# A vision tower in one program: last updates of layer 0 one per pair, and another order of work at the end of layer 1

## The chip, the cores and the metric

The kernel runs as one program on one core of a Trainium2 chip. The core has a matrix engine (TensorE, PE in the views), a vector engine (VectorE, DVE), a scalar engine (ScalarE, ACT), a general-purpose one (GpSimd, POOL) and SyncE (SP), which issues transfers (DMAs). Each engine works through its own list of instructions in order, and waits only on semaphores. TensorE writes to PSUM, of which the kernel uses eight banks; everything else lies in SBUF. The metric is the device time of one execution in microseconds (us). The profile's span, from the first instruction to the last, is somewhat shorter than that time: 1984.1 us against 1985.91 us in the profiled execution.

## The reference

32 images of 3 x 256 x 256 are cut into 256 patches each, and each patch becomes a vector of 256 numbers. Two layers follow, all in float32:

```python
h = _L0_tok_ref(x, L0_tok_W, L0_tok_b)
h = h + _L0_attn_ref(_layernorm(h, axis=-1), ...)
h = h + _L0_ffn_ref(_layernorm(h, axis=-1), ...)
h = h + _L1_attn_ref(_layernorm(h, axis=-1), ...)
h = h + _L1_ffn_ref(_layernorm(h, axis=-1), ...)
```

Three of these matter here. Layer 0's feed-forward ranks the 256 tokens of an image by a learnt weight, runs the best 127 through two matrices, and adds the results, times the weight, back at their places. Layer 1's attention is causal, over phases: two small networks, a product of phases, and a running sum. Layer 1's feed-forward has four heads with four causal experts each: softmax attention per expert, a gate that mixes the four results, a residual and a norm, two small matrices (fc1, fc2) with another norm, and a softmax over heads that scales the result:

```python
gs = jax.nn.softmax(jnp.einsum('bnsf,nef->bnse', out, gate_w) + gate_b[None, :, None, :], axis=-1)
mixed = jnp.einsum('bnsed,bnse->bnsd', out.reshape(b, nh, s, ne, d), gs)
hn = layernorm(mixed + resid, ln_g, ln_b)
...
fg = jax.nn.softmax(fout @ fgate_w.T, axis=-1)
return (fout.reshape(b, s, nh, d) * fg[..., None]).reshape(b, s, h)
```

## The kernel before

All 32 images stay in SBUF (tiles h0 to h31, two chunks of 128 tokens by 256). The stages run one after the other: patches, layer 0's attention in pairs of images, layer 0's feed-forward in quads, layer 1's attention in pairs, layer 1's feed-forward image by image. Within a stage the work of several images is interleaved, and the order of instructions on TensorE, VectorE, ScalarE, GpSimd and SyncE is the order in which the code records them; nothing is moved afterwards. So a line of the loops says for every engine at once where a piece of work stands in its queue.

**Layer 0's feed-forward, its end.** `step_c(t)` (L838) runs what the table ORDER_C lists for step t. For the last quad (images 28 to 31) three steps are left when the stage ends: END_C has `fetch` of the first half; END_C + 1 `fetch` of the second half and `update` of the first; END_C + 2 `update` of the second. `fetch` (L810) issues four gathers on GpSimd (L816), which bring an image's two chunks of results to the order of its tokens. `update` (L821) has, for two images of two chunks, three VectorE instructions each: multiply and add to h (L827), and statistics for the next norm (L123, L124); then two small GpSimd instructions turn variances into reciprocal roots (L148, L149).

**Layer 1's attention** (L966 to L1006) is a loop over t in which each pair of images starts three steps after the one before. `do(k, which)` runs a piece k steps after its pair's start: at 0 `norm_d` (VectorE, L774 to L777, makes dx), at 1 `turn` (TensorE transposes dx, L188; ScalarE copies one half to dxT, L193, VectorE the other, L195) and `residual_d` (GpSimd, L786 and L787), at 2 `hidden` (matmuls with w_wk and w_wq, activations), at 3 `phases` (L901 to L906), at 4 `match` (matmuls on dz; VectorE multiplies by the causal mask, L921), at 5 `memory` (dat,dx), at 6 `output` (matmuls wvo,dm, then statistics on VectorE, L945 and L946, and GpSimd's power d_rs), at 7 `add_output` (L955, which also frees the four banks of `output`) and `stats_e`. A step with t a multiple of 3 ends with `output`; the next one begins with `turn`. The three steps of layer 0 are run at the ends of t = 6, 7 and 8.

**Layer 1's feed-forward.** `prep` and `values` do the attention. `post(b, im, i)` (L1179) has the rest of image b in pieces i: 0 to 2 the gate (logits L1185 to L1192, softmax, then L1199 and, on GpSimd, two products of expert results and gate, L1202), 3 the mixed sum er (L1207 to L1210), 15 its squares on ScalarE (L1171), 4 their sum (L1215) and GpSimd's power (L1153, L1154), 5 the scaling (L1220), 6 the transposes (L750) and fxT (L1224), 16 a count of zeros in fxT (L1066), 7 fc1, hx (L1233) and four copies by SyncE into the tile both (L1237, L1239), 8 the matmuls with fc2 and ey (L1248), 9 and 10 squares, sum and power, 11 the scaled enorm (L1256) and the logits of the last gate, 12 transposes and foT (L1268), 13 transposes back (L1276), 14 the rest of the softmax, the product into the tile fout (L1281), the addition of h (L1285) and the output by SyncE (L1286). The pool p1 has one buffer for each name: er, fxT, hx, both, enorm, foT, fout and ex (the normed input, L754) among them. After the loop, when the last image's attention is done, the table END lists the pieces that are left as (images back from the last, piece), and

```python
for back, i in END:
    post(B - 1 - back, images[B - 1 - back], i)
```

records them in that order. Piece 10 of every eighth image is followed by `check_ranges` (L1145), two VectorE instructions over 384 numbers; their sum decides, through a flag that TensorE and VectorE finish (L1356 to L1367), whether a general version of the layer is run after all.

Of the kernel before, what the change touches and what calls it, by code (L numbers as in the profile page):

```python
# [33 lines left out]
F32 = mybir.dt.float32  # L34
# [6 lines left out]
P = 128  # L41
B, N, D = 32, 256, 256
NC = N // P
# [36 lines left out]
def vit_tower(tc, a, out):  # L80

    nc = tc.nc
# [34 lines left out]
    def over(ap, shape, axis):  # L117
        return ap.unsqueeze(axis).to_broadcast(shape)
# [422 lines left out]
    p1 = region_c.enter_context(tc.tile_pool(name="c_1", bufs=1, reuse_waits="tile"))  # L541
# [241 lines left out]
    def residual_d(b0, s):  # L783
        for j in range(2):
            h = H[b0 + j]
            nc.gpsimd.tensor_tensor(h, h, s.xs[j], ALU.add)  # L786
            nc.gpsimd.tensor_tensor(h, h, over(add_row, [P, NC, D], 1), ALU.add)  # L787

    with region_c:
# [48 lines left out]
        def step_c(t):  # L838
            for at_step, do, j in ORDER_C:
                u, r = divmod(t - at_step, 4)  # L840
                if r == 0 and 0 <= u < B // 4 and (u > 1 or do is not first_ranks):
                    do(4 * u, quads[u], j)

        END_C = 4 * (B // 4 - 1) + 4
# [20 lines left out]
    with (  # L865
# [3 lines left out]
        def turn(b0, s):  # L869
            s.xT = p2.tile([P, 2, 2 * N], F32, name="dxT")  # L870
            transposed(s.xT, s.xs, copy_split)
# [36 lines left out]
        def match(b0, s):  # L908
            s.t, ps = [], (bank(), bank())
            for key, at_q, w in ((0, 0, N), (P, P, P)):  # L910
                for i in range(2):
                    for j, p in enumerate(ps):
                        r = slice(j * 64, (j + 1) * 64)
                        q = N + at_q
                        mm(
                            p[:, 2 * key : 2 * key + w], s.z[r, i, key : key + P], s.z[r, i, q : q + w],
                            i == 0, i == 1,
                        )
            for p in ps:
                t = p8.tile([P, N + P], F32, name="dat", bufs=4)  # L920
                nc.vector.tensor_tensor(t, p[:, 0 : N + P], causal, ALU.mult)  # L921
                s.t.append(t)
# [14 lines left out]
        def output(b0, s, qs=range(2 * NC)):  # L937
            if qs[0] == 0:
                s.st, s.po = spool.tile([P, 2 * NC, 2], F32, name="d_st"), []
            for q in qs:  # L940
                m, c, p = s.m[q // NC], q % NC, bank()
                for k in range(2):
                    mm(p, m[:, k, c * P : (c + 1) * P], wvo[:, k, :], k == 0, k == 1)
                six = spool.tile([P, 6], F32, name="six")
                nc.vector.bn_stats(six, p[:, 0:D])  # L945
                nc.vector.bn_aggr(s.st[:, q, :], six)  # L946
                s.po.append(p)
            if len(s.po) == 2 * NC:
                s.rs = spool.tile([P, 2 * NC], F32, name="d_rs")
                pow_rstd(s.rs, s.st[:, :, 1])  # L950

        def add_output(b0, s):
            for q, p in enumerate(s.po):
                h = H[b0 + q // NC][:, q % NC, :]
                nc.vector.scalar_tensor_tensor(h, p[:, D:], s.rs[:, q : q + 1], h, ALU.mult, ALU.add)  # L955
# [10 lines left out]
        for t in range(3 * (NP - 1) + 8):  # L966
            def do(step, which, *more):
                u, r = divmod(t - step, 3)
                if r == 0 and 0 <= u < NP:
                    which(2 * u, pairs[u], *more)  # L970

            last = t == 3 * NP + 1
            if t != 4:
                do(1, turn)
            if not last:
                do(7, add_output)
            if t != 4:
                do(4, match)
            if last:
                output(B - 4, pairs[NP - 2], (3,))  # L980
                add_output(B - 4, pairs[NP - 2])
            do(7, stats_e)
            if t != 4:
                do(1, residual_d)
            do(2, hidden, 0)
            if t == 2:
                do(2, hidden, 1)
                turn(2, pairs[1])
            elif t == 5:
                do(2, hidden, 1, (0,))  # L990
                match(0, pairs[0])
                do(2, hidden, 1, (1,))
            else:
                do(2, hidden, 1)
            do(5, memory)
            do(3, phases)
            if t == 5:
                residual_d(2, pairs[1])
            if t > 3:
                do(0, norm_d, p8, "dx", 4)  # L1000
            if t == 3 * NP:
                output(B - 4, pairs[NP - 2], (0, 1, 2))
            else:
                do(6, output)
            if 6 <= t <= 8:
                step_c(END_C + t - 6)  # L1006
    right_d.close()
    passing_x.close()
    by_hand.close()
# [2 lines left out]
    with (  # L1012
# [129 lines left out]
        def in_range(b, first, n):  # L1142
            return ranges[:, b // 8 % 2, b % 8, first : first + n]

        def check_ranges(b):  # L1145
            r = ranges[:, b // 8 % 2, :, :].rearrange("p b x -> p (b x)")
            nc.vector.scalar_tensor_tensor(good, r, 1.0 / LOW, good, ALU.is_le, ALU.mult)
            nc.vector.scalar_tensor_tensor(good, r, 1.0 / HIGH, good, ALU.is_ge, ALU.mult)

        def head_rstd(x):  # L1150

            v = spool.tile([P, NC * NH], F32, name="hv")
            nc.gpsimd.tensor_scalar(v, x, 1.0 / HD, 1e-8, ALU.mult, ALU.add)  # L1153
            nc.gpsimd.tensor_tensor(v, v, minus_half, ALU.pow)  # L1154
            return v
# [7 lines left out]
        def softmax_rest(x, g):  # L1163
            m = spool.tile([P, g], F32, name="sm_m", tag=f"sm_m{g}")
            nc.vector.tensor_reduce(m, x, AX.X, ALU.add)
            nc.vector.reciprocal(m, m)
            nc.vector.tensor_tensor(x, x, over(m, [P, g, 4], 2), ALU.mult)  # L1167
# [6 lines left out]
        def expert_pair(im, k, at, w):  # L1174

            x, step = at[2 * k], at[2 * k + 1] - at[2 * k]
            return im.o[:, :, x : x + 2 * step].rearrange("p g (e x) -> p g e x", e=2)[:, :, :, 0:w]

        def post(b, im, i):  # L1179
# [17 lines left out]
            if i == 2:  # L1197
                softmax_rest(im.gate, NC * NH)
                nc.vector.tensor_tensor(im.gate, im.gate, im.rden, ALU.mult)  # L1199
                im.mix = [expert_pair(im, k, MIX, HD) for k in range(2)]  # L1200
                for k in range(2):
                    nc.gpsimd.tensor_tensor(  # L1202
                        im.mix[k], im.mix[k], over(im.gate[:, :, 2 * k : 2 * k + 2], [P, NC * NH, 2, HD], 3), ALU.mult
                    )
            if i == 3:
# [7 lines left out]
            if i in (4, 10):  # L1213
                ss = in_range(b, NC * NH * (NE + i // 10), NC * NH)
                nc.vector.tensor_reduce(ss, im.sq, AX.X, ALU.add)  # L1215
                im.rs = head_rstd(ss)
                if i == 10 and b % 8 == 7:
                    check_ranges(b)
            if i == 5:
                nc.vector.tensor_tensor(im.r, im.r, over(im.rs, G8, 2), ALU.mult)  # L1220
            if i == 6:
# [54 lines left out]
                        nc.tensor.transpose(im.po[:, o : o + P], im.fT[:, k, c * P : (c + 1) * P], ident)  # L1276
            if i == 14:
                softmax_rest(im.gate, NC)
                y = p1.tile([P, NC, D], F32, name="fout")
                y8 = y.rearrange("p c (n d) -> p (c n) d", d=HD)  # L1280
                nc.vector.tensor_tensor(  # L1281
                    y8, im.po.rearrange("p (g d) -> p g d", d=HD),
                    over(im.gate.rearrange("p c n -> p (c n)"), G8, 2), ALU.mult,
                )
                nc.vector.tensor_tensor(y, y, H[b], ALU.add)  # L1285
                nc.sync.dma_start(out[b].rearrange("(c p) d -> p c d", p=P), y)  # L1286
# [19 lines left out]


        END = (
            (1, 1), (1, 2), (4, 12), (2, 5), (3, 16), (0, 0), (2, 6), (1, 3), (1, 15),
            (1, 4), (0, 1), (3, 8), (3, 9), (0, 2), (1, 5), (4, 13), (4, 14), (3, 10),  # L1310
            (2, 7), (2, 16), (1, 6), (0, 3), (0, 15), (2, 8), (1, 7), (0, 4), (2, 9),
            (3, 11), (0, 5), (2, 10), (1, 16), (0, 6), (1, 8), (1, 9), (0, 7), (1, 10),
            (3, 12), (2, 11), (3, 13), (3, 14), (0, 16), (0, 8), (0, 9), (2, 12), (1, 11),
            (2, 13), (1, 12), (0, 10), (2, 14), (0, 11), (1, 13), (1, 14), (0, 12), (0, 13),
            (0, 14),
        )

        def pieces(t, table):
# [427 lines left out]
```

## Time and profile before

Three timed runs took 1986.39, 1988.32 and 1988.48 us. The profiled execution:

| engine | busy us | share |
|---|---|---|
| PE matmul | 1929.2 | 97% |
| DVE | 1308.7 | 66% |
| ACT | 821.1 | 41% |
| POOL | 721.3 | 36% |

The chain of work that ended last could be followed back only to 1922.9 us, so its shares say little of the span; listed in order of time it is of use for the end. Windows of the span, in the form start:end, length, then busy time and count of each engine, TensorE's granted clock, share and rate of DMA:

```
937.50:958.75 21.25, 21.25 (x92) 11.33 (x87) 9.47 (x22) 11.34 (x15) 0.00 (x0) 1.00 0.00 0
979.80:998.40 18.60, 13.15 (x42) 7.29 (x42) 13.27 (x40) 4.99 (x6) 6.11 (x8) 0.82 0.01 1
1009.87:1030.88 21.01, 21.01 (x90) 11.79 (x88) 11.93 (x36) 8.96 (x12) 7.41 (x8) 1.00 0.00 0
1900.00:1922.00 22.00, 22.00 (x444) 17.95 (x441) 19.87 (x60) 15.81 (x38) 9.94 (x8) 1.00 0.19 51
1922.00:1945.00 23.00, 5.23 (x54) 3.42 (x53) 19.34 (x39) 5.71 (x12) 12.89 (x9) 0.69 0.14 35
1945.00:1965.00 20.00, 12.37 (x120) 8.59 (x120) 14.22 (x43) 6.47 (x12) 7.30 (x8) 0.76 0.27 66
1965.00:1984.10 19.10, 3.46 (x14) 2.23 (x14) 7.30 (x25) 1.02 (x3) 1.44 (x1) 0.50 0.14 45
```

The order of the engines is PE, PE's weight loads, DVE, ACT, POOL. The first and the third line are undisturbed stretches of layer 1's attention: TensorE never stops. A row of a timeline gives start and length of a group of like instructions, the engine, the line of the kernel, output and inputs, shapes and count, and in brackets how long the engine had been idle and who ended that. SPq stands for the time a DMA instruction spends at the head of SyncE's queue, waits included.

### The profile page before, as it was taken

Reading aid. Unit: us, or ns where it says so; the run is one execution under the profiler, and the core shown is the slowest. Engines: PE = TensorE matmul, PEld = TensorE weight load, DVE = VectorE, ACT = ScalarE, POOL = GpSimd, SP = SyncE. Lnnn points to the kernel's source line nnn. Section 1 sums busy time; section 2 is a strip of 40 time slices with the busy share of each in tenths; the row PEclk is TensorE's granted clock in tenths of the full one; section 3 lists DMA queues with packets and bytes.
Section 4 is the critical chain, followed back from the end, with each engine's and each line's share of the span. In section 5 each row is a group of like instructions: output and inputs, shape, how many; then the busy total and the mean of one; then the engine's idle time right before and its main releaser. Section 6 shows DMA issues by size and latency. Waiting matters only on the chain. (4 is left out here: it accounts for less than half of the span.)

```text
span 1984.1 us, 37645 instructions
## 1 busy us (share of the span) xinstructions
PE 1929.2 (97%) x15108; PEld 1372.8 (69%) x15108; DVE 1308.7 (66%) x3605; ACT 821.1 (41%) x1549; POOL 721.3 (36%) x692
## 2 busy tenths in 40 slices
PE   9999999999999999999899999999999999999983
PEld 8886676666667766766555555677777777777762
DVE  2334566666686745334655655568999999999986
ACT  0002222222222122122444444477777777777761
POOL 1223234333332344234333333213443443434343
PEclk9999999999999999999999999999999999999996
DMA  8540000000000142121000000002122121212212
GB/s 300 159 144 1 0 17 32 19 19 17 17 19 14 56 128 80 51 69 40 22 1 1 0 1 0 6 18 55 45 57 53 45 66 45 63 48 55 55 39 60
DMA packets 69813, 95.09 MB, mean 48 GB/s; under 512 B 8576, under 2 KB 51200, under 8 KB 69248
## 3 DMA queue, kind: packets, MB, share of 16 engines
q1 hardware_dynamic: 62912, 75.04, 13.3%
q0 software_dynamic: 6144, 16.79, 2.8%
q8 instruction: 121, 1.98, 0.4%
q10 hardware_dynamic: 576, 0.79, 0.1%
q14 instruction: 60, 0.49, 0.1%
HBM read 46.45 MB, written 20.97 MB: 34 GB/s over the span
## 5 line engine op out<-in xcount | busy, mean ns | idle before, releaser
L1124 ACT ACTIVATE et<-bank 128x512 f32<-128x512 f32 x384 | 202.0, 598 | 73.0 <-DVE bank L1122 72.5
L115 PEld LDWEIGHTS bank<-ev,et 128*64 128x64 f32 x6144 | 197.6, 136 | 33.5 <-issue 21.4
L115 PE MATMUL bank<-ev,et 128*64 128x74 f32 (+1 forms) x6144 | 210.5, 226 | 0.0
L1122 DVE TENSOR_TENSOR bank<-bank,w_tri 128x256 f32<-128x256 f32 (+1 forms) x384 | 172.7, 513 | 51.1 <-PE bank L115 50.5
L1202 POOL TENSOR_TENSOR eo<-eo,gate 128x1024 f32<-128x1024 f32 x64 | 122.7, 1938 | 202.9 <-DVE gate L1199 168.6
L115 PE MATMUL bank<-g,sx 64*128 64x512 f32 (+1 forms) x512 | 191.2, 502 | 3.5 <-ACT g L1082 3.5
L115 PE MATMUL bank<-g,sw 64*128 64x512 f32 (+1 forms) x512 | 189.5, 502 | 0.0
L115 PE MATMUL bank<-tokW,patch 128*128 128x256 f32 x768 | 167.2, 381 | 1.8 <-DMA patch<-in_patches_dram 1.8
L115 PEld LDWEIGHTS bank<-tokW,patch 128*128 128x128 f32 x768 | 146.5, 191 | 23.0 <-issue 2.7
L115 PE MATMUL bank<-bxT,w_wuv 128*128 128x512 f32 x300 | 131.4, 592 | 0.0
L1154 POOL TENSOR_TENSOR hv<-hv,minus_half 128x8 f32<-128x8 f32 x64 | 118.5, 1852 | 5.3
L115 PE MATMUL bank<-wvo,dm 128*128 128x512 f32 x256 | 114.3, 599 | 0.0
L115 PE MATMUL bank<-w_wo,gT 128*128 128x256 f32 x512 | 113.1, 379 | 0.0
L115 PE MATMUL bank<-attn,bv 128*128 128x256 f32 x512 | 113.1, 379 | 0.0
L115 PE MATMUL bank<-w_w,hT 128*128 128x256 f32 x512 | 113.1, 379 | 0.0
L1140 ACT COPY eo<-bank 128x286 f32<-128x286 f32 x256 | 96.0, 422 | 39.0 <-PE bank L115 35.7
L115 PE MATMUL bank<-xsel,w_w 128*128 128x512 f32 x256 | 111.4, 592 | 0.0
L115 PEld LDWEIGHTS bank<-attn,bv 128*128 128x128 f32 x512 | 97.2, 190 | 19.5 <-issue 7.2
L1153 POOL TENSOR_SCALAR hv<-ranges 128x8 f32<-128x8 f32 x64 | 37.4, 585 | 198.6 <-DVE ranges L1215 198.5
L123 DVE BATCH_NORM_STATS2 six<-h 128x6 f32<-128x256 f32 x256 | 105.5, 412 | 4.4
L115 PEld LDWEIGHTS bank<-w_w,hT 128*128 128x128 f32 x512 | 96.6, 190 | 15.3 <-issue 2.9
L115 PEld LDWEIGHTS bank<-w_wo,gT 128*128 128x128 f32 x512 | 97.2, 190 | 13.2
(265 smaller groups left out, 3749.8 us busy)
## 6 DMA issues: line engine op xcount, KB each, us to landing
patch<-in_patches_dram SPq DMA_DIRECT2D x31, 768.0 KB, 4.8
sw<-sx SPq DMA_DIRECT2D x64, 128.0 KB, 2.3
both<-fxT SPq DMA_DIRECT2D x64, 128.0 KB, 2.4
both<-hx SPq DMA_DIRECT2D x64, 128.0 KB, 2.4
out_dram<-fout SPq DMA_DIRECT2D x32, 256.0 KB, 2.5
cs<-ranked SPq DMA_DIRECT2D x32, 128.0 KB, 3.2
results<-cy SPq DMA_DIRECT2D x32, 128.0 KB, 1.7
w_w<-in_w_dram SPq DMA_DIRECT2D x2, 1024.0 KB, 8.5
```

What stands on the lines that cost most here:

```text
L115: nc.tensor.matmul(o, lhsT, rhs, start=first, stop=last)
L123: nc.vector.bn_stats(six, x)
L1122: nc.vector.tensor_tensor(own, own, over(tri, [P, n_e, P], 1), ALU.add)
L1124: nc.scalar.activation(t, p, AF.Exp)
L1140: nc.scalar.copy(im.o[:, c * NH + n, 0:OC], p[:, 0:OC])
L1153: nc.gpsimd.tensor_scalar(v, x, 1.0 / HD, 1e-8, ALU.mult, ALU.add)
L1154: nc.gpsimd.tensor_tensor(v, v, minus_half, ALU.pow)
L1202: nc.gpsimd.tensor_tensor(im.mix[k], im.mix[k], over(im.gate[:, :, 2 * k : 2 * k + 2], [P, NC * NH, 2, HD], 3), ALU.mult)
```

## The change

It has four parts.

1. The three steps left of layer 0's feed-forward run at the ends of t = 6, 9 and 12 of layer 1's attention, not 6, 7 and 8: one step per pair of images, each after `output`.
2. For the last two images (b > B - 3) the two products of L1202 run on VectorE, not on GpSimd.
3. For images 27, 29 and 31 the output is made in the p1 tile named ex; images up to 26, 28 and 30 use fout as before.
4. The table END has another order, with one entry more: for the last image, `check_ranges` is a piece of its own, 17, after piece 11, where it followed piece 10.

Of the order: image 27's transposes now come before image 30's products, and its output (4, 14) after piece 9 of image 29, so behind the copies (2, 7) of image 29 in SyncE's queue, and behind piece 8 of 29. Image 30's squares (1, 9) to power (1, 10) and the transposes of the last three images stand in a slightly different order among each other.

```diff
-            if 6 <= t <= 8:
-                step_c(END_C + t - 6)
+            if t in (6, 9, 12):
+                step_c(END_C + (t - 6) // 3)
...
-                    nc.gpsimd.tensor_tensor(
+                    (nc.vector if b > B - 3 else nc.gpsimd).tensor_tensor(
...
-                if i == 10 and b % 8 == 7:
-                    check_ranges(b)
+            if i == (17 if b == B - 1 else 10) and b % 8 == 7:
+                check_ranges(b)
...
-                y = p1.tile([P, NC, D], F32, name="fout")
+
+                y = p1.tile([P, NC, D], F32, name="ex" if b > B - 6 and b % 2 else "fout")
...
         END = (
-            (1, 1), (1, 2), (4, 12), (2, 5), (3, 16), (0, 0), (2, 6), (1, 3), (1, 15),
-            (1, 4), (0, 1), (3, 8), (3, 9), (0, 2), (1, 5), (4, 13), (4, 14), (3, 10),
-            (2, 7), (2, 16), (1, 6), (0, 3), (0, 15), (2, 8), (1, 7), (0, 4), (2, 9),
-            (3, 11), (0, 5), (2, 10), (1, 16), (0, 6), (1, 8), (1, 9), (0, 7), (1, 10),
-            (3, 12), (2, 11), (3, 13), (3, 14), (0, 16), (0, 8), (0, 9), (2, 12), (1, 11),
-            (2, 13), (1, 12), (0, 10), (2, 14), (0, 11), (1, 13), (1, 14), (0, 12), (0, 13),
-            (0, 14),
+            (1, 1), (4, 12), (4, 13), (1, 2), (3, 16), (0, 0), (2, 5), (2, 6), (1, 3),
+            (1, 15), (0, 1), (3, 8), (2, 7), (1, 4), (3, 9), (0, 2), (1, 5), (3, 10),
+            (2, 16), (1, 6), (0, 3), (0, 15), (2, 8), (1, 7), (0, 4), (3, 11), (3, 12),
+            (0, 5), (2, 9), (4, 14), (2, 10), (1, 16), (0, 6), (1, 8), (1, 9), (0, 7),
+            (2, 11), (1, 10), (3, 13), (3, 14), (0, 16), (0, 8), (0, 9), (0, 10), (2, 12),
+            (1, 11), (2, 13), (1, 12), (0, 11), (0, 17), (2, 14), (1, 13), (0, 12), (1, 14),
+            (0, 13), (0, 14),
         )
```

In the changed program the lines from L1280 on are numbered one higher.

## The prediction

> **What bounds the kernel now.** I read the page first: TensorE is busy 97% of the span and its row of tenths is all nines but for one slice (the 20th) and the last two. So a microsecond can be won only where TensorE stops. The timeline of TensorE around that slice (start, length, engine, line, tiles, count, idle before it and who ended it):
>
> ```profile
> 958.75 1.04 PE L188 MATMUL bank<-ident,dx 128*128 128x128 f32 x8
> 959.72 1.58 PE L115 MATMUL bank<-dz 64*128 64x256 f32 x16
> 961.22 3.70 PE L115 MATMUL bank<-dxT,w_wk 128*128 128x512 f32 x8
> ...
> 972.78 7.13 PE L115 MATMUL bank<-wvo,dm 128*128 128x512 f32 x16
> 985.12 0.80 PE L188 MATMUL bank<-ident,dx 128*128 128x128 f32 x2 [5.20 <-DVE dx L777]
> 986.16 1.65 PE L188 MATMUL bank<-ident,dx 128*128 128x128 f32 x6 [0.25 <-DVE dx L777]
> 987.74 2.93 PE L115 MATMUL bank<-dz 64*128 64x256 f32 x16
> 990.60 4.45 PE L115 MATMUL bank<-dxT,w_wk 128*128 128x512 f32 x8
> ...
> 1009.87 1.04 PE L188 MATMUL bank<-ident,dx 128*128 128x128 f32 x8
> ```
>
> An undisturbed pair of images takes 21.0 us from one L188 to the next (1009.87 to 1030.88 later in the same view). From 958.75 to 1009.87 are two pairs in 51.12 us: **9.1 us are lost here**, 5.45 idle and the rest because the same matmuls run slower for 6 us afterwards. VectorE's timeline says why:
>
> ```profile
> 976.57 0.48 DVE L827 SCALAR_TENSOR_TENSOR h<-cx,w_kept,h 128x256 f32<-128x256 f32 x1 [5.23 <-DMA cx<-results,rank_of]
> ...
> 979.08 0.45 DVE L827 SCALAR_TENSOR_TENSOR h<-cx,w_kept,h 128x256 f32<-128x256 f32 x1
> 979.56 0.43 DVE L123 BATCH_NORM_STATS2 six<-h 128x6 f32<-128x256 f32 x1
> 980.03 0.18 DVE L124 BATCH_NORM_AGGREGATE st_d<-six 128x2 f32<-128x6 f32 x1
> ```
>
> The last update of layer 0 waits for a gather issued one step earlier, and the norm of the next pair (L777), which TensorE transposes, stands behind it on VectorE.
>
> The end is the second stop: in the windows view TensorE is busy 5.2 of the 23 us from 1922 and 3.5 of the last 19.1. Queue, product and chain lines of it:
>
> ```profile
> 1925.22 2.95 DVE L1188 TENSOR_TENSOR lg<-eo,ranges 128x64 f32<-128x64 f32 x2
> ...
> 1928.49 1.22 DVE L1207 TENSOR_TENSOR two<-eo 128x1024 f32<-128x1024 f32 x1
> ...
> 1976.48 0.69 DVE L1281 TENSOR_TENSOR fout<-bank,fgate 128x512 f32<-128x512 f32 x1 [3.97 <-DMA out_dram<-fout]
> ```
> ```profile
> 1914.12 25.92 SPq L1286 DMA_DIRECT2D out_dram<-fout  x2
> 1940.27 1.11 SPq L1237 DMA_DIRECT2D both<-fxT  x2
> ```
> ```profile
> 1942.07 3.02 DMA both<-hx
> ...
> 1972.06 4.33 DMA out_dram<-fout
> ```
>
> L1188 takes 2.95 us for two where it took 0.36 at 1920.95: GpSimd runs its products (L1202) beside it. The output of image 27 (L1286, issued at 1939.65) holds back SyncE's copies for image 29. And image 31 waits for image 30's output to leave the only fout tile.
>
> **What the Trainium skill says.** "GPSIMD Engine Reference", § 3 and § 8: elementwise work on two inputs is about twice as slow as on VectorE, and both share SBUF interfaces. The trace agrees in kind: 1.94 us mean for L1202 against 1.22 for L1207, which has as many elements (1.6 times), and L1188 above. "TensorE: Matmul & The Clock Gate", Part 1: after an idle window of some 3.4 us the clock is halved until work has lasted about as long. Here 5.20 us idle did it (2.93 for 1.58). The same page, engine queue depths: VectorE's queue is strictly first in, first out. The trace shows no overtaking.
>
> **The change, part by part.** Sums are against the profiled span, 1984.1.
>
> (a) *Steps of layer 0's end at 6, 9, 12.* Step 6 (four gathers, 5.0 us on GpSimd after d_rs) stays. Four gathers and the first update go from 7 to 9, the second update from 8 to 12. The 9.1 us go, since each update now finds data gathered a pair earlier. But the new place has a price. By the order of the built program, the 12 instructions of an update stand between the statistics of the output (L946) and the dxT copy (L195) of the next pair; in the old place at step 7 they fell into VectorE's idle time. Four times L827, L123, L124 take 4 x 1.04 = 4.16 us (979.08 to the next one at 980.12). In an undisturbed pair L195 runs at 1011.13 to 1011.79; TensorE's first matmul with dxT starts at 1012.35 and needs only the half that ScalarE copies; the second, 0.92 later at 1013.27 (3.70 for four), needs L195. With the update it can start at 1011.79 + 4.16 + 0.1 = 1016.05: a new wait of **2.8 us, twice**. Behind L195 on VectorE stand L955 (frees banks for the wq matmuls) and L921 (wanted at 1019.32 plus 2.8, ready at 1015.2 plus 4.2): both in time. 2.8 is under 3.4, so I take no loss of clock. On GpSimd the gathers and the two small power operations of the update stand behind d_rs and ahead of the statistics for layer 1's feed-forward and the residuals, which are wanted a pair or more later: nothing. Net **-9.1 + 5.6 = -3.5**. Bounds: no slack at all for TensorE (4.16 twice) gives -0.8; half the wait hidden gives -6.
>
> (b) *Products on VectorE, images 30 and 31.* Four instructions at 1.22 (row L1207) instead of 4 x 2.1 on GpSimd. They fill VectorE, but what slowed L1188, L1167 (1.51 for 0.19) and L1285 (1.58 for 0.69) is gone: 2.6 + 1.3 + 0.9 = 4.8. Both are in the walk below.
>
> (c) *New order and (d) second tile.* Walk of image 31 from 1923.8 (end of L1199 of image 30, alike in both), each term a row of this stage. VectorE now works without gaps until image 31's sum (er): four products 4.9, counts 2 x 0.67, logits 1.1 and 0.6, gate softmax 0.9, two norms of er 1.2, two sums of 2.6, ey 0.7, three L1215 1.8; with two or three waits of 0.1, 17.1: 1940.9, before 1943.5. Then squares 0.7, L1215 0.7, GpSimd's power 2.0 with hand-overs: L1220 at 1944.4, before 1950.55 (there L1215 stood behind ey of image 29, which waited for the held copies). Image 27's output and the count of image 30, which frees fxT, come first: 3.8, then fxT 0.8, fc1 matmuls 2.1 (slow clock), hx 0.75, copies 3.0, matmuls 1.9, ey 0.45: 1957.2, before 1961.6. Squares, L1215 and power 3.6: enorm at 1960.8, before 1967.23. From there VectorE's queue to the last add: enorm block 1.55, range checks 1.1 and 1.0 with small steps, outputs of 29, 30, 31 1.45 + 2.0 + 2.0: 1969.9. Image 31 now waits for image 29's output only (issue to landing 2.2 to 2.5 elsewhere): 0.5. The flag's matmul stands behind image 31's transposes on TensorE: 0 to 1.5, I take 0.5. Last add ends at **1970.9 against 1977.89: -7.0**. What follows (6.2 us to the span's end) stays. Fast clock throughout takes off another 1.9 to 2.4 (-9.4); an output that lands as late as the 4.33 above, with the flag's full 1.5, leaves -5.
>
> The range check (piece 17) now stands behind image 31's enorm instead of ahead of it; its 1.1 us are in the walk; the ex tile was read last by image 31's transposes (before 1885), so taking it costs nothing.
>
> Sum: -3.5 - 7.0 = -10.5, span 1973.6. Timed runs were 1986.39 to 1988.48 (median 1988.32); the profiled one was 1985.91. From the median: **1977.8**.
>
> **Rivals.**
> B: *the update gives back all it freed.* Each of its two places costs 4.5 us (update 4.16 and no slack). For: it is in front of the copy. Against: 1.4 us of slack counted above. Only the end pays: 1981.3.
> C: *TensorE stays fast at the end and half the new wait hides.* -6.0 - 8.5 brings 1973.8. For: at 1954 to 1965 it was fast between gaps of 2 us. Against: 4 us gaps in the walk.
> E: *VectorE becomes the bound of the end, which gains nothing*: products at GpSimd's 1.94 (4 x 0.72 = 2.9), and each of the six powers that GpSimd keeps holds VectorE up by 0.7, as its products did (4.2): 7.1, only (a) pays, 1984.8. Against: L1220, also with a broadcast input, keeps L1209's rate (0.69), and beside the power at 1933.03 VectorE's small steps kept their 0.17 to 0.20.
> D, slower: *each update stall is long enough to halve the clock.* L827 ran at 1.16 for 0.45 while GpSimd added two inputs; four such add 2.8 to the stall, 5.6, and the slow clock 3.65 as seen at 985 (9.1 - 5.45): 9.25 a step. 18.5 - 9.1 - 7.0 = +2.4: 1990.7. It decides for slower from 8.05 a step on. Against: at that place GpSimd runs powers and gathers, beside which L827 took 0.45 (966.00).
>
> **How the numbers follow.** Forecast 0.70, B 0.13, C 0.07, E 0.06, D 0.04. A measurement can tell about 0.2% (4.0 us) from no change: E and half of D fall within it. Faster 0.90, same 0.08, slower 0.02. Low end -6 - 8.5 and the spread of the runs, 1973.0; high end -0.8 - 5 from the median, 1982.5, which takes in B.
>
> **What would show it.** (a) No L777 wait of 5.2 us near 985; two waits of 2.5 to 3 us of TensorE before the second w_wk matmul, some 21 us apart, ended by L195; later matmuls at 3.70. (b) L1202 on VectorE at 1.2, L1188 at 0.18. (c) The copies of image 29 no longer wait for image 27's output; image 31's enorm starts near 1960.8 - 3.5. (d) No wait over 1 us ahead of the last L1282. Wrong: update waits above 4 us, or waits for gathers at the new places; or a last add less than 5 us earlier within the tail.

## The result, and the profile after

The changed kernel takes **1978.32 us** (median of 4 runs, 1977.45 to 1980.41) against 1987.45 us for the kernel before (4 runs): a ratio of 0.9956, 95% interval 0.9938 to 0.9973. A second set of 5 runs gave 1980.00 us and 0.9952 (0.9939 to 0.9966). The forecast was 1977.8, a gain of 10.5 us from 1988.32; between the two medians of the result lie 9.1 us.

Between the two profiled spans, 1984.1 and 1974.9 us, the 9.2 us lie as follows. The cut between the last two stretches is the end of L1199 of image 30, as in the prediction; "last add" is the end of the last addition of H to an output tile (L1285 before, L1286 after).

| stretch | before, us | after, us | difference |
|---|---|---|---|
| start to L188 of the pair before the first stall | 958.75 | 959.06 | +0.31 |
| from there, three pairs of the attention | 72.13 | 68.56 | -3.57 |
| up to the end of L1199 of image 30 | 892.93 | 893.04 | +0.11 |
| from there to the last add | 54.08 | 48.43 | -5.65 |
| last add to the end of the span | 6.21 | 5.81 | -0.40 |

The cut, image 31's enorm and the last add in VectorE's timeline of the kernel before:

```profile
1923.62 0.19 DVE L1199 TENSOR_TENSOR gate<-gate,ranges 128x32 f32<-128x32 f32 x1
...
1967.23 0.68 DVE L1256 TENSOR_TENSOR enorm<-ey,hv 128x512 f32<-128x512 f32 x1
...
1977.20 0.69 DVE L1285 TENSOR_TENSOR fout<-fout,h 128x512 f32<-128x512 f32 x1
```

First the attention. TensorE's timeline of the changed kernel (start, length, engine, line, tiles, count, idle before it and who ended it):

```profile
980.07 1.04 PE L188 MATMUL bank<-ident,dx 128*128 128x128 f32 x8
...
982.54 1.12 PE L115 MATMUL bank<-dxT,w_wk 128*128 128x512 f32 x2
986.11 2.84 PE L115 MATMUL bank<-dxT,w_wk 128*128 128x512 f32 x6 [2.44 <-DVE dxT L195]
...
1003.78 1.04 PE L188 MATMUL bank<-ident,dx 128*128 128x128 f32 x8
...
1009.95 2.84 PE L115 MATMUL bank<-dxT,w_wk 128*128 128x512 f32 x6 [2.57 <-DVE dxT L195]
```

The wait of 5.20 us is gone. Two others are there in its place, ended by the copy L195, in front of the second half of the w_wk matmuls and 23.8 us apart. The matmuls after them run at 2.84 for six, about the rate of 3.70 for eight: no loss of clock in this execution. VectorE's timeline shows what stands ahead of the copy:

```profile
981.19 0.45 DVE L827 SCALAR_TENSOR_TENSOR h<-cx,w_kept,h 128x256 f32<-128x256 f32 x1
...
985.30 0.18 DVE L124 BATCH_NORM_AGGREGATE st_d<-six 128x2 f32<-128x6 f32 x1
985.40 0.66 DVE L195 COPY dxT<-bank 128x512 f32<-128x512 f32 x1
```

L827 no longer waits for a gather, and the update takes 981.19 to 985.40, 4.21 us. Then the end, on VectorE:

```profile
1920.47 0.19 DVE L1199 TENSOR_TENSOR gate<-gate,ranges 128x32 f32<-128x32 f32 x1
1920.70 2.36 DVE L1202 TENSOR_TENSOR eo<-eo,gate 128x1024 f32<-128x1024 f32 x2
...
1923.86 0.36 DVE L1188 TENSOR_TENSOR lg<-eo,ranges 128x64 f32<-128x64 f32 x2
...
1941.26 0.69 DVE L1220 TENSOR_TENSOR er<-er,hv 128x512 f32<-128x512 f32 x1 [0.86 <-POOL hv L1154]
...
1957.95 0.69 DVE L1256 TENSOR_TENSOR enorm<-ey,hv 128x512 f32<-128x512 f32 x1 [0.87 <-POOL hv L1154]
...
1962.62 0.15 DVE L1368 CAST flag<-bank 1x1 int32<-1x1 f32 x1 [0.39 <-PE bank L115]
...
1967.67 0.69 DVE L1282 TENSOR_TENSOR ex<-bank,fgate 128x512 f32<-128x512 f32 x1 [1.91 <-DMA out_dram<-ex]
1968.40 0.69 DVE L1286 TENSOR_TENSOR ex<-ex,h 128x512 f32<-128x512 f32 x1
```

The products (L1202) take 2.36 for two here, 1.22 for each by itself, and L1188 is back from 2.95 to 0.36 for two. Image 31's enorm (the last L1256) starts 37.29 us after the cut, before 43.42. But the last output still waits: 1.91 us, where it was 3.97. SyncE's queue shows the copies of image 29 issued at once, with no output of image 27 ahead of them (before: 1940.27, behind an issue of 25.92):

```profile
1928.55 1.10 SPq L1237 DMA_DIRECT2D both<-fxT  x2
...
1943.90 0.38 SPq L1287 DMA_DIRECT2D out_dram<-ex  x1
```

And the chain that ended last names the transfer (start, length, engine or DMA, tile):

```profile
1962.77 0.60 DVE ex L1286
1963.40 4.18 DMA out_dram<-ex
1967.67 0.70 DVE ex L1282
```

Image 29's output takes 4.18 us from issue to landing. Image 31 shares its tile.

### The profile page after: what moved, and what is told of

It is laid out like the page before. It is cut to its first block, busy times and chain, and to the rows that moved or that the text cites. A ratio compares the mean times of both kernels' runs of the same rounds, so it can differ in the third digit from the quotient of the medians.

```text
span 1974.9 us, 37642 instructions
## 1 busy us (share of the span) xinstructions
PE 1929.9 (98%) x15108; PEld 1373.8 (70%) x15108; DVE 1298.0 (66%) x3609; ACT 821.4 (42%) x1549; POOL 712.4 (36%) x688
## 3 DMA queue, kind: packets, MB, share of 16 engines
q8 instruction: 121, 1.98, 0.4%
## 5 line engine op out<-in xcount | busy, mean ns | idle before, releaser
L1202 POOL TENSOR_TENSOR eo<-eo,gate 128x1024 f32<-128x1024 f32 x60 | 114.3, 1925 | 201.8 <-DVE gate L1199 201.8
L115 PEld LDWEIGHTS bank<-attn,bv 128*128 128x128 f32 x512 | 97.2, 190 | 19.6 <-issue 7.2
```

Of the source, the lines that this page charges most:

```text
L115: nc.tensor.matmul(o, lhsT, rhs, start=first, stop=last)
L1202: (nc.vector if b > B - 3 else nc.gpsimd).tensor_tensor(im.mix[k], im.mix[k], over(im.gate[:, :, 2 * k : 2 * k + 2], [P, NC * NH, 2, HD], ...
```

## The experiments

All times below are medians of the timed runs. A ratio compares a kernel with runs of the kernel before that were timed beside it, with its 95% interval in brackets; it is not the quotient of two medians, and differences in us from the kernel before are worked out from it. "After the cut" counts from the end of L1199 of image 30 in the profiled execution. A mark is a point of the work on this scale, such as the start of image 31's enorm.

### The two halves alone

Steps of layer 0's end only:

```diff
 (kernel before)
-            if 6 <= t <= 8:
-                step_c(END_C + t - 6)
+            if t in (6, 9, 12):
+                step_c(END_C + (t - 6) // 3)
```

> The kernel before with the steps of layer 0's end at 6, 9, 12 and nothing else. Theory (the update stands ahead of the dxT copy): the 9.1 us near 985 go, two waits of TensorE of 2.4 to 2.8 us ended by L195 come, net -3.2 to -3.6 us against the kernel before; the stretch from the end of L1199 of image 30 to the last add stays at 54.1 us. Rival (each place costs the whole update and more, 4.5 us): about -0.1 to -0.5 us.

Measured: 1986.68 us, ratio 0.9996 (0.9988 to 1.0005), or -0.8 us (-2.4 to +1.0). Less than the theory's -3.2, and not to be told from nothing: the median of the kernel before, timed beside it, was 1986.34. The two waits came as foretold, 2.44 and 2.55, but in this profile the first was followed by 4.54 us for the six matmuls in place of 2.84:

```profile
988.57 4.54 PE L115 MATMUL bank<-dxT,w_wk 128*128 128x512 f32 x6 [2.44 <-DVE dxT L195]
```

These are **1.70 us of slow clock** that the changed kernel's profile had not shown. The three pairs took 70.24 us, 1.9 under the kernel before. The last add came 55.43 us after the cut: the end had not become shorter.

The end only (the changed kernel, with the lines of this diff turned round):

> The changed kernel with the steps of layer 0's end back at 6, 7, 8. Theory (the parts are independent and add up): only the end pays, -5.3 to -6.3 us against the kernel before; the wait of 5.2 us near 985 and the slow matmuls after it are back; the end keeps the changed kernel's 48.4 us from the end of L1199 of image 30 to the last add. Rival (the end gained because it started from another state of clock or queues): 51 us or more there, -3 us or less.

Measured: 1979.19 us, ratio 0.9963 (0.9949 to 0.9976), -7.4 us (-10.1 to -4.8), an interval that holds the theory's -5.3 to -6.3. The last add comes 48.55 us after the cut, as in the changed kernel; the wait of 5.20 is back. The two pairs around it took 50.14 us, 8.1 more than two undisturbed ones (9.1 in the kernel before). So the end carries most of the gain, and the steps the small rest.

### The update where VectorE is idle

```diff
 (changed kernel)
-            if t in (6, 9, 12):
+            if t in (6, 10, 13):
                 step_c(END_C + (t - 6) // 3)
```

> The changed kernel with the steps of layer 0's end at 6, 10, 13 in place of 6, 9, 12: the updates then stand behind the statistics of layer 1's feed-forward, where VectorE was idle for 7.2 us. Theory (the two waits of 2.44 and 2.57 us come from the update's 4.2 us in front of the dxT copy and from nothing else): both waits go, all periods from one L188 to the next are 21.0 us, and the span is 5.0 to 5.6 us below the changed kernel's. Rival (the update costs what it costs wherever it stands, since VectorE's idle time there is needed, or the gathers on GpSimd hold back d_rs): within 2 us of the changed kernel, with a new wait ended by L901, L905 or d_rs.

Measured: 1971.21 us, ratio 0.9920 (0.9907 to 0.9934). TensorE's timeline of this kernel:

```profile
979.16 1.04 PE L188 MATMUL bank<-ident,dx 128*128 128x128 f32 x8
981.63 3.70 PE L115 MATMUL bank<-dxT,w_wk 128*128 128x512 f32 x8
...
1000.16 1.04 PE L188 MATMUL bank<-ident,dx 128*128 128x128 f32 x8
1002.64 3.70 PE L115 MATMUL bank<-dxT,w_wk 128*128 128x512 f32 x8
```

and VectorE's, where the update now starts and what follows it:

```profile
986.42 0.45 DVE L827 SCALAR_TENSOR_TENSOR h<-cx,w_kept,h 128x256 f32<-128x256 f32 x1
...
994.24 1.01 DVE L901 TENSOR_SCALAR dz<-dturn,cols 128x512 f32<-128x512 f32 x2 [2.63 <-ACT dturn L899]
```

The same line in the changed kernel:

```profile
997.87 0.88 DVE L901 TENSOR_SCALAR dz<-dturn,cols 128x512 f32<-128x512 f32 x2 [7.18 <-ACT dturn L899]
```

Both waits are gone and every pair takes 21.0 us; VectorE's idle time ahead of L901 shrank from 7.18 to 2.63 and TensorE did not wait for it. So the stalls came of the update's place. The median lies 7.1 us under the changed kernel's, which was timed at another time (7.2 by the two ratios), where the two waits of its profile account for 5.5. The rest fits the clock, next; the end was also 1.5 us shorter in this profile (46.93 after the cut), with the full clock in more of it.

### When a short wait costs clock

Of seven profiles with the steps at 6, 9, 12, five show the six matmuls behind the first wait at 4.54 us and two at 2.84, though the wait is 2.44 or 2.45 in all; the second wait, 2.55 to 2.57, never cost clock. The granted clock explains it. In every trace it changes only at multiples of 3.413 us, on a grid that lies differently in each execution. So the changed kernel was run once more, and the grid laid over both profiles. A stretch between two lines of the grid is called a window here.

> The changed kernel once more, for further runs and a second profile. Theory (the clock is granted in windows of 3.413 us, on a grid that lies differently in each execution; a wait of 2.44 us that falls into one window halves the next, one that is split by a grid line into parts of 1.8 us or less does not): the first wait at 986 is followed by 4.54 us for the six matmuls if the grid puts it into one window and by 2.84 if not, and the second wait never follows a first with loss by another loss. Rival (the loss comes from something else at that place, the gathers or GpSimd's powers): a loss with a split wait, or none with a whole one.

Measured: 1980.00 us; first wait 2.45, then 4.54 for six. The windows view of this run, cut at its own grid (stretch, length, busy time of each engine with its count, clock granted to TensorE, DMA share, GB/s):

```profile
core 0: us, PE busy (x) PEld busy (x) DVE busy (x) ACT busy (x) POOL busy (x), PEclk, DMA share, GB/s
...
983.75:987.17 3.42, 0.97 (x3) 0.49 (x3) 3.28 (x10) 0.00 (x0) 2.51 (x4) 1.00 0.27 79
987.17:990.58 3.41, 3.41 (x5) 1.33 (x4) 3.31 (x11) 0.69 (x1) 2.16 (x3) 0.50 0.28 77
1007.65:1011.06 3.41, 1.71 (x12) 0.74 (x10) 3.20 (x10) 0.63 (x1) 0.97 (x1) 1.00 0.00 0
1011.06:1014.48 3.42, 2.55 (x6) 1.25 (x7) 3.38 (x10) 0.69 (x1) 1.20 (x2) 1.00 0.01 2
```

and of the changed kernel's first profile:

```profile
980.88:984.29 3.41, 2.79 (x21) 1.59 (x18) 3.17 (x11) 1.69 (x2) 2.41 (x3) 1.00 0.01 2
984.29:987.70 3.41, 1.59 (x4) 0.87 (x5) 3.34 (x10) 0.42 (x1) 2.74 (x3) 1.00 0.38 102
987.70:991.12 3.42, 3.42 (x9) 1.51 (x8) 2.85 (x10) 1.36 (x3) 1.61 (x5) 1.00 0.19 52
```

In the rerun the first wait (983.94 to 986.39) lies in one window, which holds 2.45 us idle: the next window has clock 0.50. In the first profile a grid line at 984.29 splits the wait into 0.62 and 1.82, and the clock stays at 1.00. The second wait is split in both. All fourteen waits (two in each of the seven profiles) follow this: 2.44 or 2.45 in one window, half clock in the next (five times); parts of 1.82 or less, none (nine times). The rival (gathers or GpSimd's powers, which run beside all seven first waits) falls: the same work goes with and without the loss. It also shows why the second wait was spared: after a loss it starts 25.4 us behind the first, or 7.45 windows, which splits it; and where the first was split, the second, 23.7 us or 6.95 windows later, lies almost alike.

The grid can be laid over all thirteen traces, with a window's idle time taken as its length less the busy time of TensorE. Each of the 40 windows at full clock with 2.01 us or more idle was followed by half clock, none of some 7250 with 1.42 us or less was, and of the 38 in between 7 were. So the parts of 1.82 us or less above did no harm, but nothing says that they never could. The shortest idle time that cost clock, 1.46 us, stands in the run with the third tile (below), in a part of layer 1's feed-forward that all these kernels have alike:

```profile
1274.63:1278.04 3.41, 1.95 (x9) 0.75 (x6) 2.29 (x10) 2.72 (x4) 1.20 (x2) 1.00 0.35 82
1278.04:1281.45 3.41, 3.41 (x11) 2.88 (x12) 0.96 (x3) 1.38 (x3) 0.00 (x0) 0.50 0.00 0
```

What decides within 1.43 to 1.98 us stays open.

### Products, tile and order of the end

Products back on GpSimd:

```diff
 (changed kernel)
-                    (nc.vector if b > B - 3 else nc.gpsimd).tensor_tensor(
+                    nc.gpsimd.tensor_tensor(
```

> The changed kernel with all gate products (L1202) on GpSimd again. Theory (GpSimd's products slow what VectorE does beside them, and are longer by 0.7 to 0.9 us each): L1188, L1167 or other VectorE lines beside them take 1 us or more again, image 31's er is later by 1 to 3 us, and the span is 1 to 3 us above the changed kernel's. Rival (VectorE is the bound of the end, so that work taken from it shortens it): 0 to 2 us below the changed kernel's.

Measured: 1980.24 us, 0.9964 (0.9952 to 0.9976). VectorE's timeline shows the contention:

```profile
1923.15 3.23 DVE L1188 TENSOR_TENSOR lg<-eo,ranges 128x64 f32<-128x64 f32 x2
...
1934.01 2.41 DVE L1220 TENSOR_TENSOR er<-er,hv 128x512 f32<-128x512 f32 x1 [1.30 <-POOL hv L1154]
```

Image 31's er was done 18.62 us after the cut, against 16.75: the theory's 1.9 later. Yet enorm came at 37.43 against 37.29, since this execution had the full clock from 27.0 to 37.2 us after the cut, where the changed kernel's had half. The ratio puts it some 1.6 us above the changed kernel, within the intervals. So the delay is seen in the trace; what it costs at the end is not settled.

One tile:

```diff
 (changed kernel)
-                y = p1.tile([P, NC, D], F32, name="ex" if b > B - 6 and b % 2 else "fout")
+                y = p1.tile([P, NC, D], F32, name="fout")
```

> The changed kernel with one output tile (fout) for all images. Theory (each image waits for the landing of the one before): images 30 and 31 each wait, +1.8 us against the changed kernel if outputs land 2.3 us after their issue, +5.7 us if they take 4.2 us as image 29's did. Rival (the late landing came of two outputs in flight at once): all land in 2.1 to 2.5 us here and the loss is under 2 us. Rival (nothing waits for tiles): within 0.5 us.

Measured: 1981.36 us, 0.9969 (0.9959 to 0.9979); last add 52.54 us after the cut, 4.1 more than with two tiles. That is between the theory's +1.8 and +5.7, since image 29's output landed late and image 30's did not. VectorE's timeline:

```profile
1968.79 0.69 DVE L1282 TENSOR_TENSOR fout<-bank,fgate 128x512 f32<-128x512 f32 x1 [4.26 <-DMA out_dram<-fout]
...
1972.46 0.69 DVE L1282 TENSOR_TENSOR fout<-bank,fgate 128x512 f32<-128x512 f32 x1 [1.78 <-DMA out_dram<-fout]
```

Both last images wait. The first wait, 4.26, is for image 29's output, alone in flight: two outputs at once are not needed for a late landing.

A third tile, for image 31, from the tile of the squares:

```diff
 (changed kernel)
+                if b == B - 1:
+                    y = p1.tile(G8, F32, name="esq").rearrange("p (c n) d -> p c (n d)", c=NC)
+                else:
...
```

> The changed kernel with a third tile for the last image's output (the tile of the squares, whose last reader is done by then). Theory (the late landing of image 29's output is what held the last image): the wait of 1.91 us before the last L1282 goes, the last add ends 1.8 to 2.0 us earlier against the end of L1199 of image 30, and the span is shorter by about as much. Rival (the outputs' transfers set the end, and three in flight at once land later still): the last add comes earlier but the span gains under 0.5 us.

Measured: the wait is gone and the last add comes 46.57 us after the cut, 1.86 earlier, as the theory said. The median is 1978.66 us, 0.9956 (0.9942 to 0.9970): the timed runs don't show 1.9 us, which is less than the width of their interval. Its profiled span (1976.1) is above the changed kernel's, since its cut came 3.0 us later, in a part that both have alike; some 1.7 of this is the window of half clock at 1278.04 shown above.

The old order, with the range checks at their old place:

```diff
 (changed kernel)
-            if i == (17 if b == B - 1 else 10) and b % 8 == 7:
+            if i == 10 and b % 8 == 7:
...
-            (1, 1), (4, 12), (4, 13), (1, 2), (3, 16), (0, 0), (2, 5), (2, 6), (1, 3),
+            (1, 1), (1, 2), (4, 12), (2, 5), (3, 16), (0, 0), (2, 6), (1, 3), (1, 15),
...
```

> The changed kernel with the order of the end, and the place of the range checks, as in the kernel before; products on VectorE and two output tiles stay. Theory (the order is worth 2 us and tiles and products bring the rest): span 1 to 3 us above the changed kernel's, since ey of image 29 and image 31's L1220 stand behind each other again, but with the copies of image 29 no longer held by an output. Rival (the order carries the gain): 5 us or more above it. Rival (the order brings nothing beside the two tiles): within 0.7 us.

Measured: 1980.41 us, 0.9964 (0.9950 to 0.9978); 48.37 us after the cut. The last add is as late as in the changed kernel, as in the third case of the expectation, but the two ends had unlike clocks: of these 48.37 us TensorE had the full clock in 20.0, of the changed kernel's 48.43 in 9.1. The run with the updates at 10 and 13 has the changed kernel's end with 19.6 us of full clock, and took 46.93. So at like clock the order may bring some 1.4 us, by one profile each; the ratios can't tell. What the marks show is a trade: enorm comes at 42.45 instead of 37.29, but only 5.92 us stand between it and the last add instead of 11.14. No image waits for an output here.

Then the tile with nothing else:

```diff
 (kernel before)
-                y = p1.tile([P, NC, D], F32, name="fout")
+                y = p1.tile([P, NC, D], F32, name="ex" if b > B - 6 and b % 2 else "fout")
```

> The kernel before with the second output tile and nothing else of the change. Theory (formed from the runs with the old order and with the products on GpSimd, which both kept the end's 48 us with two tiles: the tile carries the gain and either of the others is worth nothing beside it): 48 to 49.5 us from the end of L1199 of image 30 to the last add, against 54.1 to 55.4 with one tile, no wait over 2 us ahead of the last L1282. Rival (the parts add up: one tile with new order and products kept 1.5 us of the gain, so without those the end loses 1.5 us again): 49.9 to 50.5 us. Rival (order and products can stand in for each other, but one of the two is needed): 51 us or more.

Measured: 1982.40 us, 0.9970 (0.9958 to 0.9982); 49.38 us after the cut, at the upper end of what the theory gave. Image 31 no longer waits for an output:

```profile
1970.57 0.69 DVE L1281 TENSOR_TENSOR ex<-bank,fgate 128x512 f32<-128x512 f32 x1
```

So the tile alone brings 4.70 of the end's 5.65 us. The marks of eight profiles side by side, in us after the cut; the last column has how much of the time up to the last add TensorE had the full clock:

| kernel | er of image 31 | its enorm | last add | enorm to last add | full clock |
|---|---|---|---|---|---|
| before | 19.69 | 43.42 | 54.08 | 10.66 | 17.2 |
| before, steps at 6, 9, 12 | 19.70 | 44.67 | 55.43 | 10.76 | 9.9 |
| tile only | 19.70 | 43.45 | 49.38 | 5.93 | 17.2 |
| changed, old order | 19.55 | 42.45 | 48.37 | 5.92 | 20.0 |
| changed, products on GpSimd | 18.62 | 37.43 | 48.06 | 10.63 | 16.7 |
| changed | 16.75 | 37.29 | 48.43 | 11.14 | 9.1 |
| changed, updates at 10 and 13 | 16.73 | 36.37 | 46.93 | 10.56 | 19.6 |
| changed, third tile | 16.73 | 37.31 | 46.57 | 9.26 | 9.8 |

The same end differs by some 1.4 us between executions (54.08 and 55.43, 48.43 and 46.93), and is the longer where less of the full clock was granted. No run tests that alone, but marks are best compared between rows of like clock. The tile's 4.70 is such a pair (17.2 in both). Order and products together bring 0.95 more in the changed kernel's profile, which had less of the full clock, and 2.45 in the one with 19.6 us of it; the timed runs (0.9970 for the tile only, 0.9963 for the whole end) can't tell these apart.

The order moves work from ahead of enorm to behind it: 6.1 us earlier at one mark and some 5 us longer from there, since the range checks and three outputs now stand between, and one late landing.

### The late landing

The DMA view of the changed kernel from 1963.3 to 1967.7, where image 30's output goes out too (queue and kind: packets, MB, share of 16 engines; then issues and median us to landing):

```profile
q1 hardware_dynamic: 541, 0.52, 33.7%
q8 instruction: 1, 0.02, 2.3%
q14 instruction: 1, 0.01, 0.8%
...
out_dram<-ex SPq DMA_DIRECT2D x1, 256.0 KB, 4.2
```

and of the one with the old order from 1965.2 to 1968.9, when it moves the same image's output:

```profile
q1 hardware_dynamic: 272, 0.26, 20.2%
...
out_dram<-ex SPq DMA_DIRECT2D x1, 256.0 KB, 2.1
```

In each of the eight profiles in which an image waited over 1 us for an output, an instruction packet of 16 KB (1.0 to 1.9 us long) went out during the transfer of the output behind the longest wait. In the three with two or three tiles and the old order (two above, the last one below) none ran beside image 29's output, and no image waited. The Trainium skill ("Runtime: NRT & Kernel Launch", instruction fetch mechanics) says that engines refill their instruction memory in blocks of 16 KiB over DMA queues of their own; the packets' size agrees. The coincidence goes beyond the end of the kernel. The thirteen traces have 192 outputs whose landing the profile gives, from all of layer 1's feed-forward: the 119 without an instruction packet (of 8 or 16 KB) beside them landed 2.1 to 2.6 us after issue, and all 42 that took over 2.9 us had one beside them. A packet alone is not enough: 20 of the 73 outputs with one beside them still landed within 2.7 us. That a fetch holds back the output's last packets is read from times that coincide. No run moved a fetch alone.

### The best versions

The changed kernel with updates at 10 and 13 and with the third tile:

```diff
 (changed kernel)
-            if t in (6, 9, 12):
+            if t in (6, 10, 13):
...
+                if b == B - 1:
+                    y = p1.tile(G8, F32, name="esq").rearrange("p (c n) d -> p c (n d)", c=NC)
...
```

> The changed kernel with the updates at 10 and 13 and with the third tile for the last image. Theory (the two gains are independent, and lie 900 us apart): 6.5 to 7.6 us below the changed kernel's span, some 17 us below the kernel before. Rival (one of the two is hidden behind something else): 5 us or less.

Measured: 1971.65 us, **0.9915** (0.9902 to 0.9929), 16.9 us under the kernel before. Pairs of 21.0 us and 46.57 us after the cut: both gains are in the trace, side by side. From the version without the third tile (0.9920) the timing can't tell it.

The same three tiles and updates, in the kernel before, with its order and its products on GpSimd:

```diff
 (kernel before)
-            if 6 <= t <= 8:
-                step_c(END_C + t - 6)
+            if t in (6, 10, 13):
+                step_c(END_C + (t - 6) // 3)
...
+                if b == B - 1:
+                    y = p1.tile(G8, F32, name="esq").rearrange("p (c n) d -> p c (n d)", c=NC)
...
```

> The kernel before with its order and products, three output tiles at the end and the updates at 10 and 13. Theory (tiles and the place of the updates are all that counts): within 2 us of the best version so far, that is 14 to 17 us below the kernel before; no wait of TensorE ended by L195 or L777 near 985. Rival (new order or products are needed as well): 12 us or less below it.

Measured: 1972.78 us, 0.9921 (0.9907 to 0.9935), 15.7 us under the kernel before, no wait near 985, 49.38 us after the cut. The place of the updates and the tiles make nearly all of it in the timed runs. In the traces the new order with its products still ends 2.8 us earlier (46.57 against 49.38), with less of the full clock.

## Why the prediction was right

The total was right (-10.5 forecast on the span, -9.2 measured), with two terms mis-sized, both towards too much gain. Part of the closeness is luck. The forecast of 1977.8 was counted from 1988.32, while the kernel before has 1987.45 over its four runs. And the -3.57 of the changed kernel's profile, so near to -3.5, is one of the two profiles of seven that lost no clock there.

**(a) The steps.** The mechanism held by the signs that it had named: 9.1 us went, two waits ended by L195 came. Where no clock was lost they cost 2.70 and 2.83 us a pair (periods of 23.71 and 23.84 against 21.0), forecast 2.8. The term that failed is "2.8 is under 3.4, so I take no loss of clock". A wait of 2.44 us halves the clock for 3.413 us when it falls into one window, and then costs 1.70 more; so it did in five of seven profiles. The old place lost 8.1 to 9.1 us, the new one 5.5 or 7.2: a gain of 0.9 to 3.6 in place of 3.5, and the steps alone were timed at -0.8 (-2.4 to +1.0). The lower bound of -0.8 had been set for another reason, a copy without slack, which was not what happened.

**(b), (c) The walk of the end.** Taken from the cut, its marks stood within 0.4 us: er 17.1 forecast, 16.75 measured; L1220 20.6 and 20.60; the end of ey 33.4 and 33.45; enorm 37.0 and 37.29. That they stood so near is in part luck. The terms listed for er add up to 17.7, and to 18.0 with the waits, not to 17.1; only two of the three L1215 counted (0.6 each) stand ahead of er in the trace. On the way to ey the copies took 2.2 where 3.0 was forecast, and the matmuls behind them 2.5 where it was 1.9. The share of each part was not tested by the total, and was uneven: the tile alone brings 4.70 of 5.65.

**(d) The outputs.** The mis-sized term: image 31's wait for image 29's output, forecast at 0.5 from landings of 2.2 to 2.5, was 1.91, since that output took 4.18. This breaks "no wait over 1 us ahead of the last L1282". Its 1.4 and an enorm 0.3 later, less some 0.35 in small steps, make -7.0 into -5.65. The profile of the kernel before had more of the full clock in its end than the changed kernel's; against the run with the steps alone, which has the same end as the kernel before at about the changed kernel's clock (9.9 and 9.1 us of full clock), the gain is 7.0. The late landing was in the forecast's bounds (-5), read from the 4.33 of the kernel before.

**The rivals.** B (4.5 us a place) fell as put: the waits were 2.4 to 2.6. But where the clock was lost the first place cost 4.4 (a period of 25.41), B's price for another reason, and the timed gain of the steps alone is closer to B's nothing than to 3.5. C (half the new wait hides, a fast clock at the end) did not come: the waits were 2.44 and 2.57, and in the changed kernel's first profile the granted clock was half from 19.4 us after the cut on. In the run with the updates at 10 and 13 more of the fast clock came, and the end was 1.5 us shorter. E (VectorE bounds the end and nothing is gained) fell for the whole, since 5.65 were gained, and its costs did not come: the products took 1.22, not 1.94. But that VectorE is the bound holds for the order: most of what it won ahead of enorm it gave back on VectorE's queue behind it. D (a stall costs 9.25) is excluded by the periods.

## What to carry to other kernels

A step that is moved to be fed in time must also be placed by who stands behind it: here a place some 6 us later in the pair on the same queue, in VectorE's idle time, was worth about 7 us more than the one chosen. An output tile that the next image must wait for was the first thing to double at the end of this kernel (4.70 of 5.65 us); reordering the work of a full engine moved a mark by 6.1 us and the end, at like clock, perhaps by 1.4. And take a short wait of TensorE at its length plus a chance of slow clock, not at its length.

## What the runs showed of the hardware

- The clock granted to TensorE changes only on a grid of 3.413 us, placed differently in each execution. A window with 2.01 us or more idle halved the next (40 of 40); one with 1.42 us or less did not (none of some 7250); between 1.43 and 1.98 us it went either way (7 of 38 halved). The Trainium skill ("TensorE: Matmul & The Clock Gate", Part 1) speaks of a free-running activity window and of an idle window of about 3.4 us; the traces agree on the grid and show that the window need not be idle throughout, as I had read it: 2.44 us, 72% of it, halved the clock in five of five cases.
- So one program in one place ran with and without 1.70 us of loss. A single profile of a kernel with such a wait is a sample of two cases.
- At the end of the kernel, image 29's output of 256 KB landed 2.1 us after issue, or 4.1 to 4.6 where a 16 KB instruction packet went out during the transfer. That the packet is the reason was not shown.
